# The channel gate of an AdaLN block as seven products of halves, its token sums formed one batch ahead

## The chip, the cores and the metric

One core of a Trainium2 chip runs the whole program in one launch. The metric is the device time in microseconds (us); the time of the kernel before is the median of three runs. All data and all arithmetic are float32. The engines are TensorE (PE: matrix products, PEld: its weight loads), VectorE (DVE), ScalarE (ACT), GpSimd (POOL) and SyncE (SP, which here issues most of the DMAs). Each engine takes its instructions in program order and waits for others by semaphores.

## What is computed

An AdaLN transformer block over 4 batches of 512 tokens with 512 features: a modulated layer norm, an RWKV block (time mix, then channel mix), a gated residual, a second modulated layer norm, and a mixture of experts (2 shared experts, and 16 routed ones of which each token takes 2). The part around the change is the channel mix and the residual:

```python
h = _layer_norm(x, ln2_g, ln2_b)                # x: after the time mix
hh = _time_shift(h)
kk = (h * cm_mk + hh * (1 - cm_mk)) @ Wkey.T    # 512 -> 2048
kv = jax.nn.silu(kk) @ Wval.T                   # 2048 -> 512
sr = jax.nn.sigmoid((h * cm_mr + hh * (1 - cm_mr)) @ Wcr.T)   # 512 -> 512, the gate
x = x + sr * kv
...
x = x0 + ga * x                                 # ga: one row per batch; x0: the block's input
```

## The kernel before, in words

Work is done batch by batch (b = 0 to 3), 512 tokens at a time; a batch is 4 token tiles of 128. Every engine's order is the order of the program text: the Python code emits instructions, and generators are interleaved by hand. `weave(main, back, plan)` takes one step of `main` (up to its next `yield`) and then as many steps of `back` as the plan says, one where it says nothing.

First come the time mixes of the four batches (`time_mix(b)`). Beside that of batch 3 runs `front_and_sums`: `channel_front(0)`, which makes layer norm 2 of batch 0 and its two mixed, transposed inputs `xk` (for the keys) and `xr` (for the gate), together with the sums of value weights (L553 to L556) that later products read from DRAM. The o product of batch 3 (`o_steps`, L397 to L399, products at L328) is not done there but within the gate of batch 0.

Then `channel_mix(b)` is the main generator for b = 0 to 3. Its `back` is `channel_front(b + 1)` and after it `channel_back(b - 1)`. The plan gives one step a time, but for the last batch, where after the first steps only every third yield gets one. What `channel_mix(b)` does:

- *Gate* (L596 to L614): for each of 4 token tiles a product of `xr` with `wcr`, 4 matmuls of 128 x 512 (`project_tokens`, L328), a sigmoid on ACT (L601), and on POOL the product with the gate row `ga` (L602). POOL also forms `x1 * ga + x0` for the tiles (L611 to L614). `key_terms` (L594) forms on DVE the four differences of halves of `xk` for the keys. For b = 0 the o product of batch 3 comes after the second tile: it reads `av` (L366, POOL), which waits for a reciprocal on DVE (L365) of `p` (made at L342, multiplied at L364).
- *Keys*: 4 pairs of hidden blocks; each pair is one product of 2 x 2 blocks done with seven products of halves instead of eight (the scheme of Strassen and Winograd). Banks X, Y and Z of PSUM collect them, with the pieces `kc1` (ACT copy, L624), `ku` (L675, L688), `kc5` (L679, L684) on DVE and POOL; `late` (L652 to L655) is the seventh product of a pair, put behind the first product of the next. The silu is a sigmoid (L645) and a product (L646).
- *Value*: again seven products (L705), of 16 matmuls of 128 x 256 each, `X` from A11, then T2, T1, A21, T3, A22, T4. Between them DVE forms differences of activations (L721), adds banks together (L741 to L766) and, in `result` (L728, L729), multiplies by the gate and adds onto `x1`.

`channel_back(b)` has the layer norm 3 of the batch (statistics L197 to L201, with the power on POOL at L202; `h3r` at L208 and L209), its transposes on PE (L229), the router (L861), the logits, the top two experts, counts by a small product (`ps_n`, L917), a long chain of small DVE instructions that places each token in the experts' slots (L921 to L972), a second small product (`ps_rows`, L980), and a tail (L990 to L1024).

After batch 3 come the shared experts and the 41 slots of the routed ones.

Weights and keys come through a pool of 8 buffers of 1 MB (`wpool`, tag "w"), loaded by SP some products ahead.

## Time and profile before

| | |
|---|---|
| median of 3 runs | 1048.02 us (1046.33 to 1049.45) |
| the profiled execution | 1048.66 us, of which the span of instructions is 1046.9 us |
| granted clock of TensorE | 0.991 |
| PE busy | 1013.1 us |
| DVE busy | 637.5 us |
| POOL busy | 341.4 us |
| ACT busy | 302.2 us |
| gate products (L328, ps_cr) | 128 matmul records of 592 ns |
| key products (L634, ps_ky) | 256 records of 381 ns |
| value products (L705, ps_y) | 384 records of 380 ns |

How to read the profile. A line of the timeline has the start and the length of a run of equal instructions (us), the engine, the source line, the operation, what it writes and reads, the shape and the count; in brackets it has the idle time just before, and what ended it. The mean length of one matmul record is longer than its share of the time, since matmuls are pipelined and overlap; the time that a product costs is read from the start of its first record to the start of the next product. A float32 matmul is recorded as two passes. A line of the waits has the instruction that waited, what it waited for, the sum, the count, and the longest.

### The profile page before, as it was taken

What the parts mean: (1) busy time and instruction counts of PE and PEld (TensorE: products, weight loads), DVE (VectorE), ACT (ScalarE), POOL (GpSimd) and SP (SyncE); (2) the same over time, 40 slices, a digit from 0 to 9 for tenths busy, and PEclk for the clock granted to TensorE, in tenths of its full rate; (3) what the DMA queues carried; (4) which work ended last, traced back from release to release, by engine and by line L of the source; (5) the groups of instructions that cost most, each with busy time, mean ns of one, the idle gap of its engine ahead of it and who ended that gap; (6) DMA issues with size and microseconds to landing.
All of it is one profiled execution on the core that took longest, in us unless ns stands there. A gap on an engine that the chain in (4) does not pass through costs nothing. (4 is left out here: it accounts for less than half of the span.)

```text
span 1046.9 us, 11349 instructions
## 1 busy us (share of the span) xinstructions
PE 1013.1 (97%) x3824; PEld 667.1 (64%) x3824; DVE 637.5 (61%) x1174; ACT 302.2 (29%) x490; POOL 341.4 (33%) x322
## 2 busy tenths in 40 slices
PE   7998989989999999999999999999998999999997
PEld 2443434434478886888788886888745666566643
DVE  5887998897756535665757487447646322234427
ACT  1744452624323402621143102230030222122210
POOL 2453463532463007330164006420004222041250
PEclk9999989999999999999999999999999999999999
DMA  9700130443047761356332814642443999899853
GB/s 322 242 1 2 40 101 0 131 139 125 19 173 270 280 241 66 106 204 228 111 101 75 296 41 170 239 164 81 151 152 110 326 382 383 287 331 319 283 178 114
DMA packets 96619, 182.80 MB, mean 175 GB/s; under 512 B 7512, under 2 KB 50008, under 8 KB 92464
## 3 DMA queue, kind: packets, MB, share of 16 engines
q1 hardware_dynamic: 90720, 162.92, 45.0%
q0 software_dynamic: 5840, 19.14, 5.7%
q8 instruction: 31, 0.51, 0.2%
q14 instruction: 28, 0.23, 0.1%
HBM read 149.75 MB, written 32.29 MB: 174 GB/s over the span
## 5 line engine op out<-in xcount | busy, mean ns | idle before, releaser
L202 POOL TENSOR_TENSOR rstd_ln<-rstd_ln,minus_half 128x1 f32<-128x1 f32 x64 | 42.5, 664 | 192.0 <-DVE rstd_ln L201 179.5
L705 PE MATMUL ps_y<-wval,a 128*128 128x256 f32 x384 | 85.7, 380 | 0.0
L1112 POOL DMA_INDIRECT xg<-h_d,token x41 | 39.0, 950 | 126.0 <-PE ps_down L1151 41.1
L1151 PE MATMUL ps_down<-wrt,at 128*128 128x512 f32 x164 | 77.3, 593 | 1.7 <-issue 1.7
L705 PEld LDWEIGHTS ps_y<-wval,a 128*128 128x128 f32 x384 | 72.3, 190 | 9.5
L1135 PE MATMUL ps_up<-wrt,xt 128*128 128x256 f32 x328 | 77.8, 380 | 0.1
L246 DVE SCALAR_TENSOR_TENSOR mix_ln<-hT_ln,inv,mix_ln 128x511 f32<-128x511 f32 x64 | 56.4, 924 | 17.5 <-ACT mix_ln L240 16.8
L1135 PEld LDWEIGHTS ps_up<-wrt,xt 128*128 128x128 f32 x328 | 59.1, 190 | 7.5 <-DVE xt L1129 1.1
L634 PE MATMUL ps_ky<-T,keys_hi 128*128 128x256 f32 x256 | 60.9, 381 | 2.4 <-DVE ku L675 1.3
L1129 DVE COPY xt<-ps_xt 128x512 f32<-128x512 f32 x41 | 28.3, 689 | 55.8 <-PE ps_xt L1127 42.3
L328 PE MATMUL ps_o<-wo,av 128*128 128x512 f32 x128 | 57.9, 604 | 4.2 <-POOL av L366 4.0
L634 PE MATMUL ps_kx<-mix_ln,keys_lo 128*128 128x256 f32 x256 | 60.5, 379 | 0.0
L323 PE MATMUL ps_v<-mix_ln,wv 128*128 128x512 f32 x128 | 58.8, 603 | 0.0
L323 PE MATMUL ps_r<-mix_ln,wr 128*128 128x512 f32 x128 | 57.6, 593 | 0.1
L705 PE MATMUL ps_x<-wval,a 128*128 128x256 f32 x256 | 57.4, 380 | 0.0
L705 PE MATMUL ps_z<-wval,a 128*128 128x256 f32 x256 | 57.3, 380 | 0.0
L1057 PE MATMUL ps_up_sh<-h,wsh 128*128 128x512 f32 x128 | 57.2, 593 | 0.0
L1071 PE MATMUL ps_down_sh<-wsh,mid 128*128 128x512 f32 x128 | 56.3, 594 | 0.3 <-PEq L1325 0.3
L328 PE MATMUL ps_cr<-wcr,mix_ln 128*128 128x512 f32 x128 | 55.7, 592 | 0.0
L634 PEld LDWEIGHTS ps_ky<-T,keys_hi 128*128 128x128 f32 x256 | 47.9, 190 | 10.5 <-DVE ku L675 2.4
L222 ACT ACTIVATE xn_ln<-x,nm_ln,rstd_ln 128x512 f32<-128x512 f32 x32 | 25.8, 812 | 99.6 <-DVE nm_ln L215 99.5
L365 DVE RECIPROCAL p<-p 128x512 f32<-128x512 f32 x16 | 53.6, 3353 | 0.6
(223 smaller groups left out, 1834.9 us busy)
## 6 DMA issues: line engine op xcount, KB each, us to landing
wrt<-in_rt_up_dram SPq DMA_DIRECT2D x41, 512.0 KB
wrt<-in_rt_down_dram SPq DMA_DIRECT2D x41, 512.0 KB
wval<-sums_d SPq DMA_DIRECT2D x16, 1024.0 KB
wval<-in_wval_t_dram SPq DMA_DIRECT2D x12, 1024.0 KB
keys_lo<-keys_d SPq DMA_DIRECT2D x12, 1024.0 KB
y_d<-y SPq DMA_DIRECT2D x41, 256.0 KB
keys_hi<-keys_d SPq DMA_DIRECT2D x12, 768.0 KB
mod<-mod_d SPq DMA_DIRECT2D x22, 256.0 KB
```

The lines of the kernel that those rows point to most:

```text
L202: nc.gpsimd.tensor_tensor(rstd, rstd, minus_half, ALU.pow)
L246: nc.vector.scalar_tensor_tensor(t[:, 1:], hT[:, : T - 1], inv[:, m - MK, k : k + 1], t[:, 1:], ALU.mult, ALU.add)
L323: nc.tensor.matmul(ps, w[:, k, m * P : (m + 1) * P], acts[k], start=(k == 0), stop=(k == NK - 1))
L328: nc.tensor.matmul(ps, acts[k][:, t * P : (t + 1) * P], w[:, k, :], start=(k == 0), stop=(k == NK - 1))
L365: nc.vector.reciprocal(p, p)
L634: nc.tensor.matmul(ps[:, c * HT : (c + 1) * HT], w[:, k, c * P : (c + 1) * P], acts[k], start=(fresh and c == 0 and k == 0), stop=(c == 1 ...
L705: nc.tensor.matmul(ps[:, j * HT : (j + 1) * HT], acts[p][:, c, j * P : (j + 1) * P], w[:, i, :], start=(fresh and i == 0 and j == 0), stop ...
L1057: nc.tensor.matmul(ps, wu[:, k, m * P : (m + 1) * P], h3s[b][k], start=(k == 0), stop=(k == NK - 1))
L1071: nc.tensor.matmul(ps, mids[b][j][:, t * P : (t + 1) * P], shared[j // ND][1][:, j % ND, :], start=(j == 0), stop=(j == len(mids[b]) - 1),)
L1112: nc.gpsimd.indirect_dma_start(out=xg, out_offset=None, in_=h3_d, in_offset=bass.IndirectOffsetOnAxis(ap=token[:, s : s + 1], axis=0),)
L1135: nc.tensor.matmul(ps[:, :D], xt[:, k, :], wu[:, k, :], start=(k == 0), stop=(k == NK - 1))
L1151: nc.tensor.matmul(ps, at[:, j, :], wd[:, j, :], start=(j == 0), stop=(j == ND - 1))
```

## The change

Three things change in `channel_mix`, and with them two elsewhere.

- The gate is a product of seven halves too. `xr` (features by tokens) and `wcr` are cut into 2 x 2 blocks of 256; seven products of 4 matmuls of 128 x 256 (`gate_product`) collect in banks X, Y and Z; the pieces `g1`, `g5` (ACT copies) and `gu` are summed on DVE and POOL. The four quarter results go through a sigmoid and the product with `ga` (`gate`). The seventh product is put behind the first key product (`late`). The gate has 3 yields where it had 4, and the o product for b = 0 comes after the fourth of the seven products.
- The sums of `xr`'s blocks (S1 to S4, eight DVE instructions of 128 x 256) are made in `channel_front`, so one batch ahead for b = 1 to 3, with two more yields there. The sums of `wcr`'s blocks (T1 to T4, four DVE instructions of 128 x 512) are made once, at the end of `front_and_sums`, in a tile that keeps one of the 8 weight buffers.
- `x1 * ga + x0` on POOL is done one token tile per key pair, behind the silu of `a11`.
- `result` multiplies a whole 128 x 512 quarter at once and adds it in two pieces.

```diff
         yield from mix_steps(xn, LN2_G, LN2_B, (CK, CR), channel_mixes[b], f"ln2_{b}", tag)
+        xr = channel_mixes[b][CR]
+        left = gate_sums[b] = {
+            f"A{i + 1}{j + 1}": [xr[j * NK // 2 + k][:, i * HT : (i + 1) * HT] for k in range(NK // 2)]
+            for i in range(2)
+            for j in range(2)
+        }
+        for name, one, other, op in (
+            ("S1", "A21", "A22", ALU.add),
+            ("S2", "S1", "A11", ALU.subtract),
+            ("S3", "A11", "A21", ALU.subtract),
+            ("S4", "A12", "S2", ALU.subtract),
+        ):
+            t = row_tile(f"{name}_{b}", (P, NK // 2, HT))
+            left[name] = [t[:, k, :] for k in range(NK // 2)]
+            for k in range(NK // 2):
+                nc.vector.tensor_tensor(left[name][k], left[one][k], left[other][k], op)
+            if name == "S2":
+                yield
+        yield
...
-        yield from sums
-
-    gas = {}
+        drain(sums)
+        t = wpool.tile([P, 4, NK // 2, HT], F32, tag="w", name="wcr_sums")
+        q = [wcr[:, i * NK // 2 : (i + 1) * NK // 2, j * HT : (j + 1) * HT] for i in range(2) for j in range(2)]
+        for n, one, other in ((0, q[1], q[0]), (2, q[3], q[1]), (1, q[3], t[:, 0]), (3, q[2], t[:, 1])):
+            nc.vector.tensor_sub(t[:, n], one, other)
+            wct[f"T{n + 1}"] = t[:, n]
+        yield
+
+    gas, wct = {}, {}
...
-        for t in range(NT):
-            ps = bank(f"ps_cr_{b}_{t}")
-            project_tokens(wcr, xr, t, ps)
-            yield
-            sr = row_tile(f"sr_{b}_{t}")
-            nc.scalar.activation(sr, ps, AF.Sigmoid)
-            nc.gpsimd.tensor_mul(sr, sr, ga)
-            srs.append(sr)
-            if b == 0 and t == 1:
-                yield from o_steps(B - 1)
-                key_sums(0)
-            key_terms(t)
-            if t == 0:
-                xres = [load_x(b, i, f"xr_{b}_{i}") for i in range(NT)]
-            else:
-                nc.gpsimd.tensor_mul(x1[t - 1], x1[t - 1], ga)
-                nc.gpsimd.tensor_add(x1[t - 1], x1[t - 1], xres[t - 1])
-        nc.gpsimd.tensor_mul(x1[NT - 1], x1[NT - 1], ga)
-        nc.gpsimd.tensor_add(x1[NT - 1], x1[NT - 1], xres[NT - 1])
...
+        def gate_product(ps, acts, w, fresh):
+            for k in range(NK // 2):
+                for j in range(2):
+                    nc.tensor.matmul(
+                        ps[:, j * HT : (j + 1) * HT],
+                        acts[k][:, j * P : (j + 1) * P],
+                        w[:, k, :],
+                        start=(fresh and k == 0 and j == 0),
+                        stop=(k == NK // 2 - 1 and j == 1),
+                        skip_group_check=True,
+                    )
...
+        def gate(i, j, v, out):
+            nc.scalar.activation(out, v, AF.Sigmoid)
+            both = out.rearrange("p (t o) -> p t o", t=2)
+            row = ga[:, None, j * HT : (j + 1) * HT].broadcast_to([P, 2, HT])
+            nc.gpsimd.tensor_tensor(both, both, row, ALU.mult)
+            srs[i, j] = out
+
+        left = gate_sums.pop(b)
+        xres = [load_x(b, t, f"xr_{b}_{t}") for t in range(NT)]
+        X = bank(f"ps_gx_{b}", "acc")
+        gate_product(X, left["A11"], gate_block(0, 0), True)
+        g1 = copied("g1", X)
+        Y = bank(f"ps_gy_{b}", "acc")
+        gate_product(Y, left["S2"], wct["T2"], True)
+        yield
+        gu = row_tile(f"gu_{b}")
+        nc.vector.tensor_add(gu, g1, Y)
+        Z = bank(f"ps_gz_{b}", "acc")
+        gate_product(Z, left["S1"], wct["T1"], True)
+        g5 = copied("g5", Z)
+        nc.gpsimd.tensor_add(g5, g5, g1)
+        gate_product(X, left["A12"], gate_block(1, 0), False)
+        key_terms(0), key_terms(1)
+        yield
+        gate(0, 0, X, row_tile(f"sr_{b}"))
+        if b == 0:
+            yield from o_steps(B - 1)
+            key_sums(0)
+        gate_product(Y, left["S3"], wct["T3"], False)
+        nc.vector.tensor_add(g5, g5, Y)
+        gate_product(Z, left["S4"], gate_block(1, 1), False)
+        key_terms(2), key_terms(3)
+        yield
+        gate(1, 1, g5, g5)
+        nc.vector.tensor_add(gu, gu, Z)
+        gate(0, 1, gu, gu)
+
+        def late():
+            gate_product(Y, left["A22"], wct["T4"], False)
+            nc.vector.tensor_add(g1, g1, Y)
+            gate(1, 0, g1, g1)
...
-        late = None
         for p in range(N_PAIR):
...
-            if late is not None:
-                late()
+            late()
...
             a11[p] = silu(X, f"a11_{p}", nc.vector)
+            nc.gpsimd.tensor_mul(x1[p], x1[p], ga)
+            nc.gpsimd.tensor_add(x1[p], x1[p], xres[p])
...
-        def result(t0, col, part):
-
-            at = slice(col, col + HT)
-            for j in range(2):
-                t = t0 + j
-                nc.vector.tensor_mul(srs[t][:, at], srs[t][:, at], part[:, j * HT : (j + 1) * HT])
-                nc.vector.tensor_add(x1[t][:, at], x1[t][:, at], srs[t][:, at])
+        def result(i, j, part):
+
+            sr = srs[i, j]
+            nc.vector.tensor_mul(sr, sr, part)
+            for t in range(2):
+                x = x1[2 * i + t][:, j * HT : (j + 1) * HT]
+                nc.vector.tensor_add(x, x, sr[:, t * HT : (t + 1) * HT])
```

The calls of `result` follow its new arguments, in the same places.

More of the change, by code (lines that the diff above doesn't have):

```diff
@@ L252, in adaln_block @@
     time_mixes, channel_mixes = [None] * B, [None] * B
+    gate_sums = {}
     spreads = {}
@@ L580, in channel_mix @@
         x1, ga = x1s[b], gas.pop(b)
-        srs, xres = [], []
         B11, B12, B21, B22 = [
@@ L613, in channel_mix, with copied @@
-        nc.gpsimd.tensor_mul(x1[NT - 1], x1[NT - 1], ga)
-        nc.gpsimd.tensor_add(x1[NT - 1], x1[NT - 1], xres[NT - 1])
+        def copied(name, ps):
+            t = row_tile(f"{name}_{b}")
+            nc.scalar.activation(t, ps, AF.Copy)
+            return t
+        def gate_product(ps, acts, w, fresh):
[9 more added lines that the diff above has]
+                    )
@@ new lines, in gate_block @@
+        def gate_block(i, j):
+            return wcr[:, i * NK // 2 : (i + 1) * NK // 2, j * HT : (j + 1) * HT]
+        srs = {}
+        def gate(i, j, v, out):
[6 more added lines that the diff above has]
+        xres = [load_x(b, t, f"xr_{b}_{t}") for t in range(NT)]
@@ L620, in get @@
                 quarters[b, order_of[n]] = load_quarter(b, order_of[n])
-        def copied(name, ps):
-            t = row_tile(f"{name}_{b}")
-            nc.scalar.activation(t, ps, AF.Copy)
-            return t
         a11, a12, a21, a22 = ([None] * N_PAIR for _ in range(4))
@@ L755, in channel_mix @@
         nc.vector.tensor_add(c5, c5, Y)
-        result(2, HT, c5)
+        result(1, 1, c5)
         if b + 1 < B:
@@ L762, in channel_mix @@
         nc.vector.tensor_add(u2, u2, Z)
-        result(0, HT, u2)
+        result(0, 1, u2)
         yield from product(T4, a22, Y, False)
         nc.vector.tensor_add(c1, c1, Y)
-        result(2, 0, c1)
+        result(1, 0, c1)
         channel_mixes[b] = None
```

## The prediction

> **What bounds it now.** I read the table of busy time first, then the waits of TensorE (PE), then the timelines of PE and of VectorE (DVE) at the places where the two programs differ.

> ```profile
> PE 1013.1 (97%) x3824; PEld 667.1 (64%) x3824; DVE 637.5 (61%) x1174; ACT 302.2 (29%) x490; POOL 341.4 (33%) x322
> ...
> PE ps_o L328 <- POOL av L366: 4.0, 3, 2.8
> PE ps_ky L634 <- DVE ku L675: 1.3, 2, 0.6
> PE ps_ky L634 <- DVE kc L684: 1.1, 1, 1.1
> ...
> PE ps_rows L980 <- DVE at_row L972: 0.4, 1, 0.4
> ```

> PE is busy 97% of the 1046.9 us span at a granted clock of 0.991, and all its waits sum to about 27 us. So a pass taken from PE is time gained, and a new wait of PE is time lost, one for one. PE takes its products in program order, and so does each other engine; a step put earlier on DVE delays all that stands behind it.

> **What is removed: 6.6 us of PE.** From PE's timeline, the gate of batch 1 and the product before and after it:

> ```profile
> 387.83 7.07 PE L705 MATMUL ps_y<-wval,a 128*128 128x256 f32 x32
> 394.73 13.90 PE L328 MATMUL ps_cr<-wcr,mix_ln 128*128 128x512 f32 x32
> 408.47 1.89 PE L634 MATMUL ps_kx<-mix_ln,keys_lo 128*128 128x256 f32 x8
> ```

> The gate's 32 passes of 512 columns take 408.47 - 394.73 = 13.74 us, 0.429 each. A value product's 32 passes of 256 take 6.90 us, 0.216 each: half as wide, half as long. The gate becomes 7 products of 8 such passes: 56 x 0.216 = 12.09 us. That is 1.65 us per batch, **-6.6** over four.

> [...] The value products' 0.216 us per pass, each with a weight load of its own, says that the load lies under the passes; I go by that.

> The four sigmoids stay. ScalarE (ACT) gains two copies per batch and is 29% busy. The POOL work on x1 (two of 1.27 us per token tile) goes to the key pairs, where POOL waits 3.8 to 5.0 us at L646 and L679 in batch 1's pairs: free; without that cover it would be late for a22 by at most 2.5 us a pair. The sums of weights take one of 8 weight buffers for good; SP's queue then issues loads later, but the loads of value weights run at least 20 us ahead (T4's for batch 0, issued at 348.28, is first used at 387.83): nothing, and a few us if that slack were used up.

> **Gone as well: 1.3 us.** channel_front grows by two steps, so channel_back's layer-norm steps come two steps later, no longer ahead of ku of pair 3 (batches 1 and 2): the two 0.64 us waits at L675 go. What comes late next is the following item.

> **Added: DVE work in four places where PE is near.** The sums cost 8 x 0.36 us per batch (half the 0.75 us pair of L594).

> 1. *The o product in batch 0's gate.* Now it just waits:

> ```profile
> 274.05 2.74 PE L328 MATMUL ps_o<-wo,av 128*128 128x512 f32 x6
> 277.47 11.43 PE L328 MATMUL ps_o<-wo,av 128*128 128x512 f32 x26 [0.68 <-POOL av L366]
> ```

> ```profile
> 260.52 0.75 DVE L342 TENSOR_SCALAR p<-ps_k,vec 128x512 f32<-128x512 f32 x1 [2.85 <-PE ps_k L323]
> ...
> 267.51 2.86 DVE L594 TENSOR_TENSOR T<-mix_ln 128x256 f32<-128x256 f32 x2
> ...
> 272.08 3.35 DVE L365 RECIPROCAL p<-p 128x512 f32<-128x512 f32 x1
> ```

> Ahead of L342 (p of the last head block) the change puts the 8 sums (2.9 us) and four weight sums of 128x512 (4 x 0.69 = 2.75): 5.65 us into 2.85 of idle, 2.8 late. Behind it, before the last reciprocal, come gu's add (0.69) and T3's pair (0.75). Walked through from 257.1, the reciprocal ends at 277.9 instead of 275.4. POOL, which now starts av 0.7 late behind an L602 product (to 276.15), would start it at once, so av, which the o product waits for, comes 1.8 later. On top, DVE and POOL hold each other up: the L594 pair above takes 2.86 us while POOL runs L353 and L355, 0.75 elsewhere; the new sums meet POOL's av work of 257.3 to 261 in the same way, and the T pair again. Bounds +1.8 (no blocking) to +7.4 (both groups blocked, and the gate's POOL add ahead of av); I take **+4**.
> [...]

> 2. *The second value product (T2) in batches 1 and 2.* Now:

> ```profile
> 463.80 3.62 PE L705 MATMUL ps_x<-wval,a 128*128 128x256 f32 x16
> 467.26 1.04 PE L229 MATMUL ps_t_ln<-ident,h3r 128*128 128x128 f32 x8
> 468.13 7.07 PE L705 MATMUL ps_y<-wval,a 128*128 128x256 f32 x32
> ```

> ```profile
> 465.12 0.69 DVE L655 TENSOR_TENSOR a<-a,a 128x512 f32<-128x512 f32 x1
> 465.73 2.49 DVE L721 TENSOR_TENSOR a<-a,a 128x512 f32<-128x512 f32 x4
> ```

> The T2 product reads the differences of L721. Two steps later means that DVE does statistics and h3r of one token tile (1.0 + 0.78 + 0.67, 2.45 us) between 465.73 and the first two differences, and another such step before the other two; and PE's two groups of transposes (2 x 0.87) come after T2, so PE wants it at 466.4. The first difference is ready at 465.73 + 2.45 + 0.65 = 468.8: 2.4 late. The third is ready at 468.8 + 0.6 + 2.45 + 0.6 = 472.5, where PE stands at 468.8 + 1.73 = 470.6: 1.9 more. 4.4 per batch, **+8.8**. Lower bound 3 (the two groups interleaved so that one wait is absorbed later), upper 10.5 (L209 at the 1.57 us that it takes beside POOL). Queued behind PE's wait are the transposes and T1, behind which nothing is urgent.

> 3. *The routing table (ps_rows).* Its DVE block (L921 to L972) takes 7.8 us for batch 0 and 8.8 for batch 1.

> ```profile
> 494.11 0.39 PE L917 MATMUL ps_n<-both,ahead 128*128 128x64 f32 x2
> ...
> 501.30 1.88 PE L980 MATMUL ps_rows<-at_slot,at_row 128*128 128x47 f32 x16
> ```

> ```profile
> 502.36 0.68 DVE L755 TENSOR_TENSOR c<-c,ps_y 128x512 f32<-128x512 f32 x1
> ```

> PE has two half products (6.9 us) between ps_n and ps_rows, and just fits. In the changed order ps_n stands at a product's end, so u's add and its result (0.69 + 0.69 + 0.84 = 2.2 us) are ahead of the block; PE still has 6.9 us. ps_rows then ends 10.2 us after ps_n (batch 0) and 11.1 (batch 1), against 9.1 and 9.7 from ps_n to the product behind the table now: +1.1, +1.4, and +0.7 in batch 3, where two differences go ahead. **+3.2**, bounds +0.5 (u's add moved under the product) and +5.

> 4. *The start of batch 3.* ps_rows of batch 1 now stands last before the gate, so result (2.2), the routing tail (L992 to L1024, 3.2 us) and four h3r steps (2.5 to 3.4 each) are on DVE beside the adds of the gate. Counted from the end of ps_rows: g5 += Y at 12.6 where the last gate product wants it at 12.1; gu += Z, whose bank the first key product Z needs, at 18 to 20 where PE is at 15.9; ku at 23 to 25 where PE is at 21 to 22. That is 4 to 6 us of waits against the 1.13 that goes: **+3.5**, bounds +1 (two h3r steps fast) and +5.

> **Sum.** -6.6 - 1.3 + 4 + 8.8 + 3.2 + 3.5 = +11.6. The profiled execution took 1048.66 us (span 1046.9 and 1.8 around it; the median of the three runs, 1048.02, is 0.6 below it): 1048.66 + 11.6 = **1060.3 us**. All lower bounds give -6.6 - 1.3 + 1.8 + 3 + 0.5 + 1 = -1.6, or 1047; all upper bounds -7.9 + 7.4 + 10.5 + 5 + 5 = +20, or 1069.

> **Rivals.** 0.3%, 3.1 us, is about what a measurement of this kernel tells from no change.
> - *Only the counts matter: faster, 1041.* PE's 56 short passes replace 32 long ones, the waits at L675 go, and DVE, 61% busy, finds idle time for its sums: 1048.66 - 7.9. The point that decides is whether h3r's steps lie ahead of the T2 differences; if they fell a step earlier, 8.8 us would go, and with half of the other items gone too the sum is below -3. For it: DVE has 409 us of idle time. Against: DVE's queue is in order, and its idle time does not lie at these places (0.7 us at 464.5). Chance 0.12.
> - *They cancel: 1048.* Waits at their lower bounds. Chance 0.13.
> - *DVE and POOL block each other throughout: 1068.* All added sums have two operands in SBUF, and POOL's gate products and x1 products run beside them; the 2.86 against 0.75 us row speaks for it, POOL's 33% against. Chance 0.1.
> - *The narrower passes do not pay,* so that the change removes nothing: 1067. Against it the 0.216 us row. Chance 0.02.
> - The forecast, 1053 to 1066: 0.63.

> So faster 0.12, within 0.3% 0.13, slower 0.75. The range is 1047 to 1068: it leaves out the faster case and little above.

> **What would show it.** PE's gate products at 12.1 us per batch and 0.216 per pass; new waits of PE, of ps_o on av near 3 to 6 us, of ps_y on the differences (2.4 and 1.9, in batches 1 and 2), of ps_rows on at_row, and at batch 3's start of a gate or key product on g5, gu and ku; no wait on wval or keys. I am wrong if the T2 product starts without a wait, or if the order in which DVE does h3r leaves the differences first.

## The result and the profile after

The changed kernel takes 1065.43 us (median of 4 runs, 1065.21 to 1066.55), the kernel before 1048.74 us on the same chip: a ratio of 1.0164, 95% interval 1.0144 to 1.0185. It is slower by 16.7 us where 11.6 were forecast. The profiled execution of the changed kernel took 1065.54 us, with a span of 1063.7 and a mean granted clock of 0.982 (before: 1048.66, 1046.9 and 0.991).

The page of the changed kernel, its line of busy time, and then its list of TensorE's waits (sum, count, longest):

```profile
PE 1016.7 (96%) x3920; PEld 691.5 (65%) x3920; DVE 662.3 (62%) x1210; ACT 307.1 (29%) x498; POOL 348.9 (33%) x326
```

```profile
PE ps_o L348 <- POOL av L386: 9.0, 2, 6.8
...
PE ps_y L770 <- issue: 4.9, 2, 2.5
...
PE ps_ky L699 <- DVE ku L738: 4.0, 2, 2.0
...
PE ps_rows L1045 <- DVE at_row L1037: 2.8, 3, 1.7
```

PE has *less* to do and is busy 3.6 us *longer*. The gate itself did what it was meant to. PE's timeline in batch 1 has a product every 1.73 us, as the value products have, so seven take 12.1 us in place of 13.74:

```profile
401.12 1.89 PE L630 MATMUL ps_gx<-wcr,mix_ln 128*128 128x256 f32 x8
402.85 1.89 PE L630 MATMUL ps_gy<-wcr_sums,S 128*128 128x256 f32 x8
404.57 1.89 PE L630 MATMUL ps_gz<-wcr_sums,S 128*128 128x256 f32 x8
```

The rest is waits and what follows them. PE's timeline at the four kinds of new waits: the o product in batch 0, ku and T2 in batch 1, and the routing table at the end of batch 2:

```profile
283.66 13.25 PE L348 MATMUL ps_o<-wo,av 128*128 128x512 f32 x26 [6.75 <-POOL av L386]
...
460.36 2.76 PE L699 MATMUL ps_ky<-T,keys_hi 128*128 128x256 f32 x8 [2.01 <-DVE ku L738]
462.91 2.86 PE L699 MATMUL ps_kz<-mix_ln,keys_hi 128*128 128x256 f32 x8
465.60 3.62 PE L770 MATMUL ps_x<-wval,a 128*128 128x256 f32 x16
...
476.82 7.40 PE L770 MATMUL ps_y<-wval,a 128*128 128x256 f32 x32 [2.42 <-issue]
...
650.61 2.63 PE L1045 MATMUL ps_rows<-at_slot,at_row 128*128 128x47 f32 x16 [1.66 <-DVE at_row L1037]
653.02 3.44 PE L630 MATMUL ps_gx<-wcr,mix_ln 128*128 128x256 f32 x8
```

Look at what comes *behind* each wait. The 26 passes of the o product take 13.25 us, where they took 11.43 before; the key products at 460.36 and 462.91 take 2.55 and 2.69 us to the next start, not 1.73; the gate product at 653.02 takes 3.28. The granted clock says why. The same place in windows of 2 us (length, PE's busy time, records, granted clock, share of the DMA engines, GB/s):

```profile
458.00:460.00 2.00, 0.35 (x2) 1.00 0.00 0
460.00:462.00 2.00, 1.64 (x6) 0.86 0.03 8
462.00:464.00 2.00, 2.00 (x6) 0.50 0.00 0
464.00:466.00 2.00, 2.00 (x8) 0.79 0.00 0
466.00:468.00 2.00, 2.00 (x11) 1.00 0.35 109
```

About 1.1 us after PE took up work again, its clock is halved for some 3.4 us. This wait of 2.0 us costs 3.8.

The wait of T2 is put down to `issue`, which means nothing that the profile shows. VectorE's lines fit it: the differences that T2 reads (L786) stand behind a layer-norm step, the first of the two is ready at about 476.7, half-way through its line, and the product starts at 476.82.

```profile
475.37 0.75 DVE L209 SCALAR_TENSOR_TENSOR h3r<-h3r,rstd_ln,mod 128x512 f32<-128x512 f32 x1
476.03 1.29 DVE L786 TENSOR_TENSOR a<-a,a 128x512 f32<-128x512 f32 x2
```

By stage, from gate to gate, in the two profiled executions (us):

| stage | before | after | difference |
|---|---|---|---|
| start to the gate of batch 0 | 267.19 | 267.26 | +0.1 |
| batch 0 | 127.54 | 133.86 | +6.3 |
| batch 1 | 118.71 | 124.48 | +5.8 |
| batch 2 | 119.32 | 127.42 | +8.1 |
| batch 3 | 118.64 | 117.41 | -1.2 |
| shared and routed experts | 295.5 | 293.27 | -2.2 |

Only batch 3, where no new wait of length appears, is shorter. Its 1.2 us are not the gate's gain alone: beside that gain of 1.65 the wait of 1.13 on kc is gone, and the half clock at its start costs 1.6.

### The profile page after: what moved, and what is told of

It is laid out like the page before. It is cut to its first block, busy times and chain, and to the rows that moved or that the text cites. A ratio compares the mean times of both kernels' runs of the same rounds, so it can differ in the third digit from the quotient of the medians.

```text
span 1063.7 us, 11599 instructions
## 1 busy us (share of the span) xinstructions
PE 1016.7 (96%) x3920; PEld 691.5 (65%) x3920; DVE 662.3 (62%) x1210; ACT 307.1 (29%) x498; POOL 348.9 (33%) x326
## 5 line engine op out<-in xcount | busy, mean ns | idle before, releaser
L246 DVE SCALAR_TENSOR_TENSOR mix_ln<-hT_ln,inv,mix_ln 128x511 f32<-128x511 f32 x64 | 64.2, 1044 | 24.8 <-ACT mix_ln L240 24.4
L343 PE MATMUL ps_v<-mix_ln,wv 128*128 128x512 f32 x128 | 58.2, 597 | 0.0
L343 PE MATMUL ps_r<-mix_ln,wr 128*128 128x512 f32 x128 | 57.5, 592 | 0.0
L770 PEld LDWEIGHTS ps_x<-wval,a 128*128 128x128 f32 x256 | 48.4, 190 | 8.1 <-issue 1.7
```

What stands on the lines that cost most here:

```text
L246: nc.vector.scalar_tensor_tensor(t[:, 1:], hT[:, : T - 1], inv[:, m - MK, k : k + 1], t[:, 1:], ALU.mult, ALU.add)
L343: nc.tensor.matmul(ps, w[:, k, m * P : (m + 1) * P], acts[k], start=(k == 0), stop=(k == NK - 1))
L770: nc.tensor.matmul(ps[:, j * HT : (j + 1) * HT], acts[p][:, c, j * P : (j + 1) * P], w[:, i, :], start=(fresh and i == 0 and j == 0), stop ...
```

## The experiments

**Theory A:** the added steps and sums put VectorE's and ACT's work in a worse order, PE waits, and behind a wait of some 2 us the clock is halved for a while (3.4 us behind the 2.01 on ku, above). **Rival B:** the seven narrow products and their adds cost the time wherever they stand. Rival D is told with its run. Each ratio is against runs of the kernel before on the same chip.

### One part alone: x1 on POOL

```diff
             a11[p] = silu(X, f"a11_{p}", nc.vector)
+            nc.gpsimd.tensor_mul(x1[p], x1[p], ga)
+            nc.gpsimd.tensor_add(x1[p], x1[p], xres[p])
```

This is in the kernel before; the same two lines are taken out of the gate's loop.

> The kernel before with one part of the change alone: x1 times the gate row, plus the input, moved from the gate to the key pairs on POOL. Theory A: the 1.13 us wait on kc in batch 3, which POOL's queue makes, goes, and nothing else moves: 0 to 1.5 us less, no change that can be told. Rival: POOL comes late with a22 and a21 in the key pairs and the time rises by 2 us or more.

Measured: 1049.22 us, ratio 0.9991 (0.9978 to 1.0005): no difference. The 1.13 us wait on kc is gone and batch 3 takes 117.23 us in place of 118.64. This part is innocent.

### Does a wait cost more than its length?

```diff
             u2 = row_tile(f"ku_{b}_{p}")
+            if b in (1, 2) and p == N_PAIR - 1:
+                for i in range(2):
+                    nc.vector.tensor_add(row_tile(f"probe_{b}_{i}"), c1, c1)
             nc.vector.tensor_add(u2, c1, Y)
```

p2_stall and p6_stall are the kernel before, with two (as here) or six extra adds that nobody reads.

> The kernel before the change with two extra 128 x 512 adds on VectorE (written to scratch rows that nobody reads) ahead of ku in pair 3 of batches 1 and 2: TensorE's 0.64 us waits there become about 2.0 us, the length that the changed kernel shows. Theory A: each is followed by about 3.4 us at half clock, so the two cost 2 x 1.4 of wait and up to 2 x 1.7 of clock, 4.5 to 6.2 us more than before. Rival D (the lower clock of the changed kernel has another cause, its narrower passes or its load, and a wait costs only its own length): 2.8 us more and the clock stays at 1.00 there.

Measured: 1055.34 us, ratio 1.0069 (1.0043 to 1.0095). The waits became 2.92 us, 2.28 longer (two adds at the 0.69 us of L655 would have made it 1.4), and batches 1 and 2 took 122.43 and 123.25 us, 3.7 and 3.9 longer: 1.4 and 1.7 us beyond the wait. PE's timeline there:

```profile
457.40 3.43 PE L634 MATMUL ps_ky<-T,keys_hi 128*128 128x256 f32 x8 [2.92 <-DVE ku L678]
460.67 1.89 PE L634 MATMUL ps_kz<-mix_ln,keys_hi 128*128 128x256 f32 x8
```

The first product behind the wait takes 3.27 us, the next 1.72. This kernel has no narrow gate products and no added sums, so rival D falls: the wait itself brings the half clock.

> As p2_stall, with six extra adds ahead of ku in pair 3 of batches 1 and 2. Theory A: the two waits become 6 to 8 us each, and the loss of clock behind each stays what it was, about 1.7 us (3.4 us at half clock, since the clock comes back after a fixed stretch of work): batches 1 and 2 longer by the wait's growth plus 1.5 to 1.9 us. Rival (the clock falls further, or for longer, the longer the wait): more than 2.5 us of clock behind each.

Measured: 1062.45 us, ratio 1.0116 (1.0098 to 1.0134). The waits are 5.3 us, 4.7 longer; the batches are longer by 7.5 each. The clock costs 2.8 us behind each, not 1.5 to 1.9: the expectation of theory A was wrong here, and the rival's held. That the clock comes back after a fixed stretch was my assumption, and no run shows it: by the windows of 2 us the stretch at half clock is 3.4 us around the waits of p2_stall and 6.8 around these. The windows show that the clock falls within the wait, at about 457, and stays at half for the first 5.7 us of the work:

```profile
454.00:456.00 2.00, 0.00 (x0) 1.00 1.00 342
456.00:458.00 2.00, 0.00 (x0) 0.83 0.78 303
458.00:460.00 2.00, 1.59 (x4) 0.50 0.00 0
460.00:462.00 2.00, 2.00 (x7) 0.50 0.14 51
462.00:464.00 2.00, 2.00 (x6) 0.50 0.21 80
464.00:466.00 2.00, 2.00 (x10) 0.97 0.00 0
```

### Undo the added steps

```diff
-            if name == "S2":
+            if name == "S2" and b == 0:
                 yield
-        yield
+        if b == 0:
+            yield
...
         gate_product(Y, left["S3"], wct["T3"], False)
+        yield
         nc.vector.tensor_add(g5, g5, Y)
```

> The changed kernel, but the token sums of batches 1 to 3 take no steps of their own in channel_front and the gate has four yields again, so that channel_back's steps stand where they stood before the change. Batch 0 is left as changed. Theory A (the added steps put layer norm 3 and the routing block ahead of what TensorE waits for, and each such wait of about 2 us or more halves the granted clock for about 3.4 us after it): the 2.4 us waits of the T2 product, the 0.8 and 1.7 us waits of the routing product and the 2.0 us waits on ku go (a wait on ku of up to 1 us may stay), the batches 1 and 2 come down from 124 and 127 us to 117 to 119, and the time to 1048 to 1051 us. Rival B (the seven products with 256 columns and their adds cost the time themselves, wherever the steps stand): batches 1 and 2 stay above 122 us and the time above 1060.

Measured: 1057.96 us, ratio 1.0076 (1.0045 to 1.0107), between the two. The waits of T2 and of ps_rows in batches 1 and 2 are gone, as theory A has it, and the batches are at 121.43 and 120.34 us; but all eight sums now stand in one step ahead of ku; ku, behind a layer-norm step as before the change, comes later, and its wait grew from the 0.64 of before to 2.50:

```profile
465.80 3.01 PE L701 MATMUL ps_ky<-T,keys_hi 128*128 128x256 f32 x8 [2.50 <-DVE ku L740]
```

So the steps explain T2 and the table; the sums need a place of their own. Batch 0, whose code is as in the changed kernel, took 136.06 us in this profiled execution, the longest of five (1053.86 to 1062.01), with a wait of 7.97 on av where the changed kernel's trace has 6.75; the run of e7 below shows how one code can have two such waits.

### Free the o product: three covers, one behind the other

```diff
-        for name, one, other, op in (
...
+        for name, one, other, op in GATE_SUMS[: 2 if b == 0 else 4]:
...
         yield
+        if b == 0:
+            flush()
         gu = row_tile(f"gu_{b}")
...
         if b == 0:
-            yield from o_steps(B - 1)
+            for t, _ in enumerate(o_steps(B - 1)):
+                if t == 0:
+                    for name, one, other, op in GATE_SUMS[2:]:
...
+                            nc.vector.tensor_tensor(left[name][k], left[one][k], left[other][k], op)
+                    wct.pop("rest")()
+                yield
```

`wct["rest"]` forms T3 and T4; `flush` issues the last division.

> The changed kernel, but in batch 0 the sums S3, S4, T3 and T4 are formed on VectorE beside the o product, and the last division is put ahead of the gate's add and the key terms; nothing else moves. Theory A: the 6.75 us wait of the o product falls below 1 us and the halved clock after it (1.7 us) goes: about 7.8 us less, 1057 to 1058. [...]

Measured: 1061.47 us, ratio 1.0123 (1.0101 to 1.0145), and batch 0 is at 133.56 us, where the changed kernel has 133.86. Nothing was won there; the median is 4 us lower all the same, and the profiled execution, the longest of the four (1065.12), does not show where. Theory A's 1057 to 1058 did not come out: the wait on av shrank to 1.49 us, and a wait of 5.06 on something else came out from behind it.

```profile
277.94 1.12 PE L349 MATMUL ps_o<-wo,av 128*128 128x512 f32 x2 [1.49 <-POOL av L387]
284.12 12.07 PE L349 MATMUL ps_o<-wo,av 128*128 128x512 f32 x24 [5.06 <-ACT sr L650]
```

The second o tile takes the bank that the sigmoid of the first quarter frees, and on ACT that sigmoid is queued behind a layer-norm activation that waits for a late statistic of VectorE (in e4's trace, with the same wait of 5.06, ACT idles 8.37 us for it, and the sigmoid follows at 284.06). The edit itself made it later: the sigmoid ends 17.3 us after the start of the gate, in the changed kernel 13.7. So the changed kernel had this cover too, but a shorter one.

The next kernel joins the two, and forms the sums of batch b + 1 where VectorE idled for 7.1 us, behind T2's differences:

```diff
         yield from product(T2, a11, Y, True)
+        if 1 <= b < B - 1:
+            token_sums(b + 1, GATE_SUMS)
```

For b = 0 the same call stands behind the sixth value product.

> Both together, and the token sums of the next batch formed not beside the keys but where VectorE idles: behind the T2 value product's differences in batches 1 and 2 (7 us idle in the kernel before), at the end of batch 0. Theory A: gate -6.6 against the kernel before, the waits on ku of batches 1 and 2 as before (0.64) or less, no wait of the o product, T2 or the routing product above 0.7 us, clock 0.99: 1039 to 1043 us, faster than before. Rival B: above 1048.

Measured: 1049.11 us, ratio 1.0013 (0.9998 to 1.0029). Batches 1 and 2 are at 117.07 and 117.72 us, 1.6 below the kernel before: that is the gate's gain, whole, and so rival B falls, although the time is where it put it, 6 us above theory A's range. No wait of T2 is left, of the table only the 0.43 of before in batch 3, and ku's is 0.64 again. But batch 0 still has 133.80, and batch 3 has 118.28, hardly less than the 118.64 before: the gate's 1.65 and the 1.13 on kc are gained there, but a new wait of 0.73 on gu and 1.7 us of half clock behind the table take most of it back. Then the second cover:

```diff
         key_terms(0), key_terms(1)
+        if b == 0:
+            gate(0, 0, X, row_tile(f"sr_{b}"))
         yield
-        gate(0, 0, X, row_tile(f"sr_{b}"))
+        if b:
+            gate(0, 0, X, row_tile(f"sr_{b}"))
```

> e4 with one more step moved: in batch 0 the sigmoid of the first gate quarter is issued ahead of channel_front's step, so ahead of the layer-norm activation xn on ACT that waits for a statistic of VectorE; it frees the bank that the second o product needs. Theory A2 (in the changed kernel two covers lay over the o product, the late av and the late bank, and e2 and e4 took away only the first): the 5.06 us wait on ACT sr goes, the wait on av of about 1.3 us stays, batch 0 falls from 133.8 to 126 to 128 us, the time to 1041 to 1044, faster than before by 0.4 to 0.7%. Rival (the o product is held by something third, such as the copies or POOL): batch 0 stays above 130 and the time above 1046.

Measured: 1051.23 us, ratio 1.0016 (1.0004 to 1.0029), batch 0 at 133.05. The wait on sr went and a third one took its place: the third o tile needs the bank that the add of the first one frees, and that add stands behind the key terms and the sums that e2 had moved there. Those sums are 2.5 us of VectorE's time (282.55 to 285.10 in e6's trace), so most of the 4.17 us wait is e2's own making. The rival was right about the time.

> e5, and the weight sums T1 and T2 formed some steps earlier beside batch 3's time mix, where VectorE waits 3.4 us for ACT. Theory A2: the last block's p comes 1.5 to 2.3 us earlier on VectorE, the wait on av (1.3 us) falls below 0.3, batch 0 at 125.5 to 126.5, the time 1 to 2 us below e5's, 1040 to 1043. Rival: VectorE's delay there falls on the k and v products instead (new waits of TensorE at L343's products), and nothing is won.

The edit forms T1 and T2 at the eighth step of `channel_front(0)`. Measured: 1049.64 us, ratio 1.0003 (0.9990 to 1.0016); the wait on av falls to 0.35, batch 0 to 131.41, and no new wait shows at the k and v products. The time is 1.6 below e5's, as expected, but not at 1040 to 1043, since the third cover is as long as in e5:

```profile
278.19 4.56 PE L344 MATMUL ps_o<-wo,av 128*128 128x512 f32 x10 [0.35 <-POOL av L382]
286.91 8.52 PE L344 MATMUL ps_o<-wo,av 128*128 128x512 f32 x16 [4.16 <-DVE x L415]
```

```diff
-        key_terms(0), key_terms(1)
+        if b:
+            key_terms(0), key_terms(1)
...
-                if t == 0:
+                if t == 2:
                     token_sums(b, GATE_SUMS[2:])
                     wct.pop("rest")()
+                    key_terms(0), key_terms(1)
```

> e6, and in batch 0 the key terms T1 and T3 and the sums S3, S4, T3, T4 go behind the second add of the o product instead of ahead of its first one. Only two banks are left for the o product's four tiles beside the gate's three, so its third tile waits for the add of its first. Theory A3 (the o product had three covers, one behind the other: av, the bank that the sigmoid frees, the bank that the add of the first tile frees; each stands behind the added work in an engine's queue): the 4.16 us wait on the add goes and no wait above 0.7 us takes its place; batch 0 falls from 131.4 to 125 to 127 us, its share 127.54 - 1.65 and less; the time to 1043 to 1046 us, faster than before by 0.3 to 0.6%. Rival: a fourth cover shows, batch 0 stays above 129 and the time at 1049.

Measured: 1039.47 us, ratio 0.9921 (0.9901 to 0.9941): faster than the kernel before, by more than was expected. No wait on the add is left. The profiled execution is the longest of the six (1048.01) and shows a wait of 2.04 us on av, with the clock halved behind it and batch 0 at 128.98; the next kernel (e8) has 0.35 in the same code. The two traces show why. In batch 3's time mix PE waits for a layer norm. In e7's profiled execution the product behind that wait ran at full clock, in e8's at half:

```profile
236.11 0.52 PE L229 MATMUL ps_t_ln<-ident,xn_ln 128*128 128x128 f32 x3 [2.53 <-DVE nm_ln L215]
237.10 3.17 PE L339 MATMUL ps_k<-mix_ln,wk 128*128 128x512 f32 x7
240.54 0.60 PE L229 MATMUL ps_t_ln<-ident,xn_ln 128*128 128x128 f32 x4
...
281.01 13.12 PE L344 MATMUL ps_o<-wo,av 128*128 128x512 f32 x26 [2.04 <-POOL av L382]
```

```profile
233.98 0.52 PE L229 MATMUL ps_t_ln<-ident,xn_ln 128*128 128x128 f32 x3 [2.93 <-DVE nm_ln L215]
234.98 5.29 PE L339 MATMUL ps_k<-mix_ln,wk 128*128 128x512 f32 x8
240.11 0.60 PE L229 MATMUL ps_t_ln<-ident,xn_ln 128*128 128x128 f32 x4
```

The product takes 3.44 us to the next start in e7 and 5.13 in e8. So in e7 PE came to the o product 1.69 us earlier against VectorE, and it waited 1.69 us longer there: a half clock that comes or stays away at one wait sets the length of a later one. Batch 0 is 3.4 us longer than in e8; what else sets this execution 8.5 us above the median, and why the median is below the expected range, no trace shows. Then the wait on ku:

```diff
             key_product(Y, k[S2], terms["T2"], True)
-            yield
+            if p < N_PAIR - 1:
+                yield
             u2 = row_tile(f"ku_{b}_{p}")
             nc.vector.tensor_add(u2, c1, Y)
+            if p == N_PAIR - 1:
+                yield
```

> e7, and in pair 3 the add that makes ku stands ahead of the yield, so ahead of channel_back's layer-norm step: VectorE may wait for TensorE there, but TensorE no longer for ku. Theory A: the 0.64 us waits of batches 1 and 2 go, 1.0 to 1.5 us less than e7 in the sum of the two batches; in the time this is at the edge of what can be told. Rival (the layer-norm step then comes late for the transposes or the differences): a new wait there of 0.6 us or more, and no gain.

Measured: 1040.30 us, ratio 0.9919 (0.9899 to 0.9938). The two waits on ku are gone, and batches 1 and 2 take 116.16 and 116.81 us, 0.9 less each than with e7; in the time the two can't be told apart. Batch 0 is at 125.60, which is 127.54 less 1.65 and 0.3 of a shorter wait:

```profile
275.80 2.74 PE L344 MATMUL ps_o<-wo,av 128*128 128x512 f32 x6
278.89 11.43 PE L344 MATMUL ps_o<-wo,av 128*128 128x512 f32 x26 [0.35 <-POOL av L382]
290.15 1.89 PE L642 MATMUL ps_gy<-wcr_sums,S 128*128 128x256 f32 x8
```

## Why the prediction was right, and where it was not

The sign and the range held, and the mechanism in kind: PE gained 6.6 us, and VectorE's order lost more. In size there was luck: the errors of the single terms nearly cancelled, and 8.7 us of halved clock, which the sum left out, still fell within the range. The experiments show the mechanism from both sides, since the same seven products with the steps put elsewhere are 0.8% faster than the kernel before. Step by step:

- *Gate, -6.6.* Right: 1.73 us per product, 12.1 per gate; e4's batches 1 and 2 are 1.6 shorter.
- *ku, -1.3.* Wrong in sign. The waits grew from 0.64 to 2.01 us, +2.7. The step saw the layer-norm work leave VectorE's queue ahead of ku, but not that S3 and S4 take its place, and that they meet POOL: in batch 1 the pair at 457.22, beside POOL's add of 457.33 to 458.75, took 1.81 us and the other 0.75, where 0.75 each was reckoned.
- *The o product, +4.* The wait grew by 6.1, within the bounds, near the blocked end. VectorE's line shows it: three of the four pairs of sums took 1.8 us, beside three POOL instructions between 257.81 and 263.15; the fourth, begun at 263.36, took 0.75.

```profile
257.58 1.77 DVE L334 TENSOR_TENSOR S<-mix_ln,mix_ln 128x256 f32<-128x256 f32 x2
259.28 1.82 DVE L334 TENSOR_TENSOR S<-S,mix_ln 128x256 f32<-128x256 f32 x2
```

  The step named only av; behind it were two more covers (e2, e5), which av's wait hid, if shorter ones than e2 and e5 show.
- *T2, +8.8.* The order was right, the size was not: two waits of 2.42 and 2.48, and 0.34 within each product, 5.6 in all. The first wait is the 2.4 that was worked out. The second was an error of mine in counting: a T2 product has 8 passes for each of four differences, 1.73 us, so the third difference is wanted 3.45 us after the first, not 1.73, and is only 0.2 to 0.3 late.
- *ps_rows, +3.2.* Right in the sum: the waits and the longer table come to 3.1 in the three batches. They split as 1.3, 1.9 and -0.1, where 1.1, 1.4 and 0.7 were reckoned.
- *Batch 3, +3.5.* Wrong here: no wait, and the 1.13 on kc went. The step took L209 at 1.57 us, its length beside POOL's x1 products, which the change had moved away; it took 0.75 in the first two of the four steps. With e2, waits of 1.22 on gu and 1.17 on ku do appear at that place. In the changed kernel's own trace the first gate products run at half clock there, which gives VectorE 1.6 us more; that this alone hid the waits is argued, not shown.
- *What the sum left out: the clock.* After the waits, PE's products run at half clock: +1.8 behind the o product, 1.8 behind each wait on ku, 1.8 and 1.6 behind ps_rows, 8.7 us in all. That is why PE is busy 3.6 us longer: -6.6 and 8.7 make 2.1 of it; the other 1.5 I did not trace. The prediction reckoned a wait at its own length. The trace of before would have told otherwise: in its windows the clock is at 0.50 behind the longer waits at 82, 144, 147 and 232 us (2.83, 2.23, 2.14 and 2.94), and at 1.00 behind the 0.64 us ones.

```profile
144.00:146.00 2.00, 1.05 (x2) 0.69 0.00 0
146.00:148.00 2.00, 0.80 (x1) 0.50 0.00 0
148.00:150.00 2.00, 2.00 (x4) 0.50 0.00 0
150.00:152.00 2.00, 2.00 (x4) 0.60 0.00 0
```

So the waits were forecast at 18.2 us and came to about 16.4, with errors on both sides that nearly cancelled, and the clock added 8.7; the experts' 2.2 us less is the spread of that stage (293.2 to 297.1 over these profiled executions).

## What to carry to other kernels

Where TensorE is the bound and every queue is in order, a change that saves its passes is paid or lost by where its helper instructions stand; look for the stretch in which the helper's engine idles (here 7.1 us behind T2's differences) and put them there. A wait can hide others of the same product: take its operands and its banks one by one, and ask of each what releases it, before reckoning what removing one cover brings. And price a wait of TensorE with the clock behind it: here one of 2 to 8 us cost 1.4 to 2.8 us more than its length when it brought the half clock.

## What was not expected of the hardware

It is not a sharp limit: the wait of 2.42 us ahead of T2 left the clock at 1.00 in the changed kernel, and the same wait in e2 halved it; the wait of 2.00 on ku in e2 did not, that of 2.01 one batch later did. Behind ps_rows, whose products have 47 columns, the clock fell to one half after waits of 0.80 and 1.66 us in the changed kernel; after the same waits of 0.79 and 1.67 in e2 it stayed at 1.00. After the wait of 0.43 there in batch 3 it fell in e1 and in e4 to e8, and in none of the kernel before, x1_only, p2_stall and p6_stall; why, the traces do not tell.
